# The last two blocks of a two-layer attention kernel: additions, residual, checks and GpSimd's drain rearranged

## The chip, the cores and the metric

The kernel runs on one core of a Trainium2 chip. The metric is the device time of one execution in microseconds (us), given as the median of several runs. Beside it stands one execution recorded by the hardware profiler: its span from the first to the last instruction, and every instruction and transfer in it.

A core has TensorE (PE, matrix products; its weight loads are listed as PEld), VectorE (DVE), ScalarE (ACT), GpSimd (POOL) and SyncE (SP). In this kernel SP does nothing but issue DMAs, and GpSimd mostly issues those DMAs that add to their destination.

## The reference

Input x has 16 images of 256 channels and 32 by 32 positions. Two layers follow each other, each adding attention to its input:

```python
x = x + attention_0(group_norm(x))
x = x + attention_1(group_norm(x))
```

In a layer, with 4 heads of 64 channels and n = 1024 positions:

```python
q, k, v = (W @ xf + b, split into heads)
sim  = einsum('bhdi,bhdj->bhij', q, k)
qpos = einsum('hdi,bhdj->bhij', rel_h + rel_w, q)
attn = softmax(sim + qpos, axis=-1)
out  = einsum('bhdn,bhmn->bhdm', v, attn)
```

All numbers are 32-bit floats.

## The kernel before, in words

**Units and blocks.** A unit is one layer of one image; there are 32 of them (list `units`). Each has two pairs of heads (`pr`), and each pair is done in two halves of 512 query positions. So there are 128 blocks `(u, pr, half)`, numbered n = 0 to 127. The last four are 124 and 125 (unit 31, pair 0; written 31_0 below) and 126 and 127 (unit 31, pair 1; 31_1). Unit 31 is layer 1 of image 15, and unit 30 that of image 14. In the traces 31_0 and 30_1 name such pairs.

**One block.** For each j of 8 tiles of keys, VectorE writes the position term into a PSUM tile (`seed`, L349), TensorE adds the product of q and k (`scores`, L385), and ScalarE writes the exponential to p (L394). For some tiles of the last blocks TensorE makes the position term too, out of `wide` (argument `tag` of `scores`), and no seed is needed. VectorE adds the eight p together (`add_up`, L403 for the first addition, L405 for the rest; the result is `acc`). TensorE multiplies v with p into `po` (`attend`, L419) in two stretches, `values_of_p(0)` and `values_of_p(1)`; between them GpSimd sets a token (L166) as a signal that the first stretch is done. ScalarE takes `po` out (`take_out`, L480).

**Sums.** The softmax's denominators are the sums of `acc` over its 128 rows. In most blocks GpSimd's adding DMAs fold them (L436, L441, L460, L465), and SP spreads the result into `den_all` (L473). In the last blocks TensorE sums the rows with a matrix of ones (`sums_of_p`, L490), ScalarE copies the sums into `d` (L500) and SP spreads them into `den_all` (L504). `reciprocals` then takes the reciprocals on VectorE (L515), sends them to DRAM (L517) and back, copied over 64 rows each (L522), into `rden`.

**The end of a pair.** `finish` multiplies the output with `rden` (`normalise`, L530) and adds bias and residual (`add_residual`, L537), both on VectorE; in layer 1 SP then stores the result (L539).

**Order.** The order of instructions on each engine is that of the program (a manual schedule): an engine runs its instructions in turn, and a waiting one holds all behind it. The order around the change is written out by hand in `block` and, for blocks 126 and 127, where no work on a next unit is left, in `block_without_pieces` (L758). PSUM tiles come from four tags `f0` to `f3`; a tile of a tag can be written when the reader of the one before is done.

**Block 126 before.** Additions 5 to 7 of block 125; scores 1 to 3; the sums of 31_0 (L772) and their spreading; reciprocals of 30_1 (`before`); the first additions, a seed for tile 7; scores 4 to 6 with `wide`; reciprocals of 31_0; first stretch of values; `finish` of 30_1; seeds for block 127, additions 5 and 6; second stretch of values.

**Block 127 before.** Addition 7 of block 126, the sums of block 126, `finish` of 31_0, additions, scores, first stretch of values; then the last addition, the sums over rows of this block into `pd` (L565), a reciprocal of all 512 columns at once (L813), the second stretch of values, sums over columns (L574) for the check, the second half of the output (L551, L552), then the checks.

**The checks.** `in_range` (L558 to L560) tests that all denominators lie between two bounds. The results go to `good`, are reduced to one number and written to `flag` (L822), which all engines load at L1194. If the flag says that a denominator was out of range, a general path runs instead (L1195, not taken here). L1223 is the line of the frame around the program: the drains and the barrier that end it.

Of the kernel before, what the change touches and what calls it, by code (L numbers as in the profile page):

```python
# [17 lines left out]
P = 128  # L18
# [34 lines left out]
def fast_path(ctx, tc, sh, x, layers, out, W, den_all, token, good, flag):  # L53
# [290 lines left out]
    def seed(blk, j, tag):  # L344

        u, pr, half = blk
        ps = psum2(tag, f"ps_{u}_{pr}_{half}_{j}")
        ab = abt[u, pr][:, :, j, :]
        nc.vector.tensor_tensor(  # L349
            ps.rearrange("p h (w y) -> p h w y", y=H),  # L350
            ab[:, :, :H].unsqueeze(2).to_broadcast([P, 2, XH, H]),
            ab[:, :, H + half * XH : H + (half + 1) * XH]
            .unsqueeze(3)
            .to_broadcast([P, 2, XH, H]),
            ALU.add,
        )
        seeds[blk, j] = ps
# [15 lines left out]
    def scores(blk, j, tag=None):  # L373

        u, pr, half = blk
        ps = psum2(tag, f"ps_{u}_{pr}_{half}_{j}") if tag else seeds.pop((blk, j))
        columns = slice(half * HALF, (half + 1) * HALF)
        for x, c in enumerate(QUARTERS):
            for h, hs in enumerate(QUARTERS):
                j0 = j * P + x * D  # L380
                terms = [(ks[u, pr], qs[u, pr])]
                if tag:
                    terms = [(qs[u, pr], wide[u, pr])] + terms
                for i, (a, b) in enumerate(terms):
# [12 lines left out]
    def add_up(blk, j):  # L397
        u, pr, half = blk
        if j == 0:
            return  # L400
        if j == 1:
            accs[blk] = apool.tile([P, 2, HALF], F32, tag="acc", name=f"acc_{u}_{pr}_{half}")
            nc.vector.tensor_tensor(accs[blk], probs[blk, 0], probs[blk, 1], ALU.add)  # L403
        else:
            nc.vector.tensor_tensor(accs[blk], accs[blk], probs[blk, j], ALU.add)  # L405
# [69 lines left out]
    def take_out(blk, po):  # L475

        u, pr, half = blk
        if half == 0:
            outs[u, pr] = opool.tile([P, 2, HALF], F32, tag="od", name=f"od_{u}_{pr}", bufs=3)
        nc.scalar.copy(  # L480
            outs[u, pr][:, half, :].rearrange("p (a n) -> p a n", a=2), po[:, :, :QUART]
        )

    def sums_of_p(two, po):

        for a in range(2):
            for x, blk in enumerate(two):
                for h in range(2):
                    r0 = (2 * x + h) * R
                    nc.tensor.matmul(  # L490
                        po[r0 : r0 + R, a, QUART:],
                        W.ones[:, :R],
                        accs[blk][:, h, a * QUART : (a + 1) * QUART],
                        start=True, stop=True, tile_position=(0, r0), skip_group_check=True,
                    )

    def keep_sums(po, n, count):
        rows_ = slice(0, 2 * count * R)
        d = ppool.tile([P, 2, HALF], F32, tag="p", name=f"d_{n}")[:, 0, :]
        nc.scalar.copy(d[rows_].rearrange("p (a n) -> p a n", a=2), po[rows_, :, QUART:])  # L500
        for x in range(count):
            for h in range(2):
                r0 = (2 * x + h) * R
                nc.sync.dma_start(  # L504
                    den_all[h * D : (h + 1) * D, n + x, :], d[r0 : r0 + 1, :]
                )

    def reciprocals(u, pr, count=2):

        n = index[u, pr, 0]
        r8 = fpool.tile([P, 2, 8], F32, tag="r8", name=f"r8_{u}_{pr}")
        nc.vector.reciprocal(r8[:, :count, :], den_all[:, n : n + count, :])  # L515
# [16 lines left out]
    def add_residual(u, pr):  # L532
# [5 lines left out]
        if l == NL - 1:  # L538
            nc.sync.dma_start(flat(out[b, pr * P : (pr + 1) * P]), xs)  # L539

    def finish(u, pr):
        normalise(u, pr)
        add_residual(u, pr)
# [15 lines left out]
        yield nc.vector.scalar_tensor_tensor(t, den, DEN_HI, t, ALU.is_le, ALU.mult)  # L559
        yield nc.vector.tensor_reduce(good[:, i : i + 1], t, AX.X, ALU.min)  # L560

    def sums_on_rows(acc, pd):

        for h, c in enumerate(QUARTERS):
            nc.tensor.matmul(  # L565
                pd[c, 0, :], W.ones[:, :D], acc[:, h, :],
                start=True, stop=True, skip_group_check=True,
            )

    def sums_on_columns(acc, pd):  # L570

        for h in range(2):
            for e in range(HALF // P):
                nc.tensor.matmul(  # L574
                    pd[:, 4 * h + e : 4 * h + e + 1],
                    acc[:, h, e * P : (e + 1) * P],
                    W.ones[:, :1],
                    start=True, stop=True, skip_group_check=True,
                )


# [37 lines left out]
    def block(n):  # L619
# [109 lines left out]
            spread_sums(*stacked)  # L729
        if half == 1 and u + 3 < NU and units[u + 3][1] == 0 and u > 0 or n == 3:  # L730
            load_x(units[u + 3][0], range(pr_, pr_ + 1) if u > 0 else range(CC))
        if half == 0:
            add_up(blk, 5)
        if before:
            finish(*before)
# [22 lines left out]
    def block_without_pieces(n, half):  # L758

        blk = blocks[n]  # L760
        u, pr, _ = blk
        f0, f1, f2, f3 = ring
        summed = blocks[n - 2][:2] if half == 0 else (u, pr)
        before = blocks[n - 4][:2] if half == 0 else blocks[n - 3][:2]
        first = index[summed + (0,)]
        if half == 0:
            add_up(blocks[n - 1], 5)
            add_up(blocks[n - 1], 6)
        add_up(blocks[n - 1], 7)
        for j in range(1, 4):  # L770
            scores(blk, j)
        sums_of_p(blocks[first:n], pos[n - 1])  # L772
        keep_sums(pos[n - 1], first, n - first)
        if half == 1:
            finish(*before)
        else:
            reciprocals(*before)
        add_up(blk, 1)
        seed(blk, 7, f2)
        add_up(blk, 2)  # L780
        add_up(blk, 3)
        for j, tag in ((4, f1), (5, f0), (6, f1)):
            scores(blk, j, tag)
        reciprocals(*summed, n - first)
        scores(blk, 7)
        add_up(blk, 4)
        if half == 0:
            seed(blocks[n + 1], 0, f0)
        po = pos[n] = psum2(f3, f"po_{n}")
        values_of_p = attend(blk, po)  # L790
        values_of_p(0)
        if half == 0:
            finish(*before)
            scores(blocks[n + 1], 0)
        if half == 0:
            seed(blocks[n + 1], 1, f1)
            seed(blocks[n + 1], 2, f2)
        add_up(blk, 5)
        if half == 0:
            seed(blocks[n + 1], 3, f0)  # L800
        add_up(blk, 6)
        if half == 0:
            values_of_p(1)
            take_out(blk, po)
            return
        add_up(blk, 7)
        acc = accs.pop(blk)
        pd = psum2(f0, "pd")
        sums_on_rows(acc, pd)
        values_of_p(1)  # L810
        finish_half(u, pr, 0, outs[u, pr][:, 0, :], rdens[u, pr][:, :HALF])
        rden = rdens[u, pr][:, HALF:]
        nc.vector.reciprocal(rden, pd[:, 0, :])  # L813
        pd = psum2(f2, "pd_columns")[:, 0, : 2 * HALF // P]
        sums_on_columns(acc, pd)
        finish_half(u, pr, 1, po[:, :, :QUART], rden)
        list(in_range(flatden[:, 8 * checked : 8 * n], 1))
        list(in_range(pd, 2))
        nc.vector.tensor_reduce(good[:, 3:4], good[:, 0:3], AX.X, ALU.min)
        pc = psum2(f1, "pc")[0:1, 0, 0:1]  # L820
        nc.tensor.matmul(pc, good[:, 3:4], W.ones[:, 0:1], start=True, stop=True)
        nc.vector.tensor_copy(flag, pc)  # L822
# [404 lines left out]
```

## Time and profile before

| What | us |
|---|---|
| Median of 3 runs | 2545.81 |
| Lowest and highest run | 2545.58, 2547.84 |
| The profiled execution | 2544.62 |
| Its span | 2542.9 |

Busy time in some stretches at the end, from the profile's sums by stretch:

| Stretch, us from the start | PE | DVE | ACT | POOL |
|---|---|---|---|---|
| 2440 to 2460 (20 long) | 20.00 | 18.70 | 10.80 | 6.91 |
| 2489 to 2510 (21 long, block 126) | 19.95 | 17.83 | 10.74 | 0.21 |
| 2510 to 2530 (20 long, block 127) | 16.09 | 19.48 | 7.77 | 0.09 |
| 2530 to 2543 (13 long) | 2.96 | 3.56 | 0.00 | 0.00 |

How to read the views: times are us from the start of the span. In the chain of waits a line is start, length, and what ran; "issue" is time in which nothing is waited for that the profile shows. In the timeline a line is start, length, engine, line of code, operation, output<-input, shape, count, and in brackets the idle time before it with what ended it. Drains, branches and waits for semaphores are run by an engine's sequencer (a q behind the engine's name) and aren't counted as busy. A matmul in fp32 is recorded as two.

### The profile page before, as it was taken

Reading aid. Unit: us, or ns where it says so; the run is one execution under the profiler, and the core shown is the slowest. Engines: PE = TensorE matmul, PEld = TensorE weight load, DVE = VectorE, ACT = ScalarE, POOL = GpSimd, SP = SyncE. Lnnn points to the kernel's source line nnn. Section 1 sums busy time; section 2 is a strip of 40 time slices with the busy share of each in tenths; the row PEclk is TensorE's granted clock in tenths of the full one; section 3 lists DMA queues with packets and bytes.
Section 4 is the critical chain, followed back from the end, with each engine's and each line's share of the span. In section 5 each row is a group of like instructions: output and inputs, shape, how many; then the busy total and the mean of one; then the engine's idle time right before and its main releaser. Section 6 shows DMA issues by size and latency. Waiting matters only on the chain.

```text
span 2542.9 us, 86134 instructions
## 1 busy us (share of the span) xinstructions
PE 2514.2 (99%) x37474; PEld 1335.6 (53%) x37474; DVE 2269.4 (89%) x2135; ACT 1949.5 (77%) x3874; POOL 835.1 (33%) x1194
## 2 busy tenths in 40 slices
PE   8999999999999999999999999999999999999997
PEld 4555555555555555555555555555555555555554
DVE  6888998989989889899898898998998998989997
ACT  6778777787777887777877778877778777787753
POOL 1332333323333233333233332333333333323320
PEclk9999999999999999999999999999999999999999
DMA  3344444454444444444444444445445444443441
GB/s 90 70 83 81 77 91 75 78 110 93 87 97 97 87 83 86 95 84 87 100 87 86 88 96 83 83 96 101 82 96 107 81 79 91 75 82 76 86 91 59
DMA packets 119537, 221.05 MB, mean 87 GB/s; under 512 B 53736, under 2 KB 55272, under 8 KB 119152
## 3 DMA queue, kind: packets, MB, share of 16 engines
q0 software_dynamic: 53568, 129.58, 30.7%
q1 hardware_dynamic: 65584, 85.90, 12.2%
q8 instruction: 295, 4.83, 0.8%
q14 instruction: 90, 0.74, 0.1%
HBM read 51.78 MB, written 17.30 MB: 27 GB/s over the span
## 4 chain that ended last, share of the span: by engine, by line
PE 94%; DVE 2%; POOL 1%; issue 1%; DMA 1%; SPq 0%; ACT 0%; POOLq 0%; DVEq 0%; ACTq 0%
PE po L419 33%; PE ps L385 33%; PE pv L298 8%; PE pk L268 8%; PE pq L268 8%; PE pa L326 2%; DVE acc L405 1%; DVE ps L349 1%; POOL rstd L237 1%; DMA stack<-stack 0%; POOL stack L465 0%; POOL stack L460 0%; PE pm L209 0%; DMA x<-in_x_dram 0%; DMA rden<-rd 0%
## 5 line engine op out<-in xcount | busy, mean ns | idle before, releaser
L349 DVE TENSOR_TENSOR ps<-abt 128x1024 f32<-128x1024 f32 x1018 | 1226.8, 1228 | 235.3 <-ACT p L394 147.7
L394 ACT ACTIVATE p<-ps,shift 128x1024 f32<-128x1024 f32 x1024 | 1092.2, 1114 | 323.4 <-PE ps L385 320.5
L385 PE MATMUL ps<-q,k 64*64 64x512 f32 x8192 | 985.5, 590 | 0.8 <-DVE ps L349 0.8
L419 PE MATMUL po<-p,v 64*64 64x256 f32 x16384 | 930.7, 376 | 2.1 <-POOL token L166 2.1
L419 PEld LDWEIGHTS po<-p,v 64*64 64x64 f32 x16384 | 628.9, 133 | 367.2 <-issue 76.9
L405 DVE TENSOR_TENSOR acc<-acc,p 128x1024 f32<-128x1024 f32 x644 | 783.3, 1216 | 7.1
L385 PEld LDWEIGHTS ps<-q,k 64*64 64x64 f32 x8192 | 308.5, 133 | 395.7 <-issue 275.1
L465 POOL DMA_DIRECT2D stack<-stack x310 | 249.6, 805 | 338.7 <-DMA stack<-stack 277.6
L166 POOL MEMSET token<- 1x1 f32 x320 | 35.8, 112 | 830.4 <-PE po L419 400.7
L460 POOL DMA_DIRECT2D stack<-acc x248 | 223.2, 1098 | 71.9 <-DMA stack<-acc 44.1
L298 PE MATMUL pv<-Wv,xn 64*64 64x256 f32 x4096 | 244.4, 376 | 1.6 <-POOL token L166 1.4
L268 PE MATMUL pq<-xn,Wq 64*64 64x512 f32 x2048 | 244.3, 592 | 0.3 <-DVE xn L913 0.3
L268 PE MATMUL pk<-xn,Wk 64*64 64x512 f32 x2048 | 242.8, 589 | 0.0
L248 ACT ACTIVATE xn<-x,nshift,rstd 128x128 f32<-128x128 f32 x496 | 209.9, 495 | 18.2 <-POOL nshift L239 18.2
L298 PEld LDWEIGHTS pv<-Wv,xn 64*64 64x64 f32 x4096 | 153.3, 133 | 104.3 <-issue 48.3
L190 ACT ACTIVATE junk<-x,neg 128x128 f32<-128x128 f32 x498 | 195.1, 401 | 0.0
L436 POOL DMA_DIRECT2D acc<-p x124 | 115.5, 931 | 227.8 <-ACT od L480 128.5
L441 POOL DMA_DIRECT2D acc<-acc x124 | 109.5, 883 | 206.0 <-DMA acc<-p 197.0
L480 ACT COPY od<-po 128x512 f32<-128x512 f32 x127 | 74.4, 586 | 118.9 <-PE po L419 118.9
L403 DVE TENSOR_TENSOR acc<-p,p 128x1024 f32<-128x1024 f32 x128 | 156.3, 1221 | 0.0
L268 PEld LDWEIGHTS pq<-xn,Wq 64*64 64x64 f32 x2048 | 78.6, 134 | 142.1 <-issue 136.7
L190 ACT ACTIVATE junk<-x 128x128 f32<-128x128 f32 x480 | 144.8, 311 | 0.0
(74 smaller groups left out, 1118.8 us busy)
## 6 DMA issues: line engine op xcount, KB each, us to landing
acc<-p POOLq DMA_DIRECT2D x124, 512.0 KB, 5.1
rden<-rd SPq DMA_DIRECT2D x126, 256.0 KB, 4.1
acc<-acc POOLq DMA_DIRECT2D x124, 256.0 KB, 3.6
x<-in_x_dram SPq DMA_DIRECT2D x32, 512.0 KB, 5.1
stack<-acc SPq DMA_DIRECT2D x248, 64.0 KB, 2.1
stack<-acc POOLq DMA_DIRECT2D x248, 64.0 KB, 3.3
out_dram<-x SPq DMA_DIRECT2D x31, 512.0 KB, 5.1
stack<-stack POOLq DMA_DIRECT2D x62, 128.0 KB, 2.9
```

The source lines that it names most:

```text
L190: nc.scalar.activation(junk, grouped(xt[units[u][0]], g), func, accum_out=into[:, g : g + 1], **bias)
L248: nc.scalar.activation(grouped(xns[u], g), grouped(xt[units[u][0]], g), AF.Identity, bias=shift[:, g : g + 1], scale=rstd[:, g : g + 1],)
L268: yield nc.tensor.matmul(pk[c, nh, :], w[l][rs, cc, c0 : c0 + D], xns[u][rs, cc, nh * HALF : (nh + 1) * HALF], start=(t == 0 and cc == 0), ...
L298: yield nc.tensor.matmul(pv[c, a, i, :], xns[u][rs, cc, j0 : j0 + D], W.wv[l][rs, cc, :], start=(t == 0 and cc == 0 and i == 0), stop=(t = ...
L349: nc.vector.tensor_tensor(ps.rearrange("p h (w y) -> p h w y", y=H), ab[:, :, :H].unsqueeze(2).to_broadcast([P, 2, XH, H]), ab[:, :, H + h ...
L385: nc.tensor.matmul(ps[c, h, :], a[hs, j0 : j0 + D], b[hs, columns], start=bool(tag) and i == 0, stop=i == len(terms) - 1, skip_group_check ...
L394: nc.scalar.activation(p, ps, AF.Exp, bias=W.shift)
L403: nc.vector.tensor_tensor(accs[blk], probs[blk, 0], probs[blk, 1], ALU.add)
L405: nc.vector.tensor_tensor(accs[blk], accs[blk], probs[blk, j], ALU.add)
L419: yield nc.tensor.matmul(po[c, a, :QUART], vts[u][rs, j, c0 : c0 + D], p[rs, h, a * QUART : (a + 1) * QUART], start=(t == 0 and j == 0), s ...
L460: nc.gpsimd.dma_start(at, acc[R:D, h, :], accum_op=ALU.add)
L465: nc.gpsimd.dma_start(stack[:rows_], stack[rows_ : 2 * rows_], accum_op=ALU.add)
```

## The change

All of it lies in `block_without_pieces`, but for one line in `block`; two small functions are new.

- **Block 125**: its addition 5 is made in the block itself, ahead of `finish`, and not at the start of block 126.
- **Block 126**: scores 4 stand ahead of the sums of 31_0. The reciprocals of 30_1 come first in SP's queue, then the spreading of the sums of 31_0 and its reciprocals. 30_1 is finished in another way: VectorE multiplies (`normalise`), ScalarE adds the bias to x in place, and a DMA issued by GpSimd adds the product to x (`add_by_dma`). Additions 5 to 7 of block 126 move to the start of block 127. After the DMA GpSimd runs a drain.
- **Block 127**: SP stores the x that the adding DMA completed (`store`). The checks of the denominators up to block 123 move to the start of the block. The last addition falls away: `sums_on_rows` takes `acc` and p of tile 7 and adds both on TensorE. `finish` of 31_0 moves behind the last addition. The sums over columns fall away: ScalarE copies `pd` into `d`, and SP spreads it into `den_all` by two DMAs, from where the last check reads blocks 126 and 127.

The built program's order shows besides that ScalarE's copy of `pd` waits for VectorE's reciprocal of `pd`, and that SP's store of x of image 14 stands between the spreading of the sums of block 126 and the reciprocals of 31_1.

```diff
+    def add_by_dma(u, pr):
+        b, l = units[u]
+        xs = xt[b][:, pr, :]
+        nc.scalar.activation(xs, xs, AF.Identity, bias=W.bv[l][:, pr : pr + 1])
+        nc.gpsimd.dma_start(xs, outs.pop((u, pr)).rearrange("p a n -> p (a n)"), accum_op=ALU.add)
+
+    def store(u, pr):
+        b = units[u][0]
+        nc.sync.dma_start(flat(out[b, pr * P : (pr + 1) * P]), xt[b][:, pr, :])
...
+    def sums_on_rows(parts, pd):
+        for i, part in enumerate(parts):
+            for h, c in enumerate(QUARTERS):
                 nc.tensor.matmul(
+                    pd[c, :], W.ones[:, :D], part[:, h, :],
+                    start=i == 0, stop=i == len(parts) - 1, skip_group_check=True,
                 )
...
-        if half == 0:
+        if half == 0 or n == len(blocks) - 3:
             add_up(blk, 5)
...
+        last = half == 1
+        previous = blocks[n - 1]
+        summed = previous[:2]
         first = index[summed + (0,)]
+        before = blocks[n - 4][:2]
+        for j in range(5 if last else 6, NT):
+            add_up(previous, j)
         for j in range(1, 4):
             scores(blk, j)
+        if last:
+            sums_of_p(blocks[first:n], pos[n - 1])
+            keep_sums(pos[n - 1], first, n - first)
+            store(*blocks[n - 5][:2])
+            list(in_range(flatden[:, 8 * checked : 8 * first], 1))
         add_up(blk, 1)
         seed(blk, 7, f2)
+        if not last:
+            reciprocals(*before)
         add_up(blk, 2)
         add_up(blk, 3)
+        scores(blk, 4, f1)
+        if last:
+            add_up(blk, 4)
+            reciprocals(*summed, n - first)
+        else:
+            sums_of_p(blocks[first:n], pos[n - 1])
+            keep_sums(pos[n - 1], first, n - first)
+        scores(blk, 5, f0)
+        scores(blk, 6, f1)
+        if last:
+            add_up(blk, 5)
+            add_up(blk, 6)
         scores(blk, 7)
         po = pos[n] = psum2(f3, f"po_{n}")
         values_of_p = attend(blk, po)
+        if not last:
+            after = blocks[n + 1]
+            seed(after, 0, f0)
+            add_up(blk, 4)
+            values_of_p(0)
+            scores(after, 0)
+            values_of_p.word()
+            seed(after, 1, f1)
+            seed(after, 2, f2)
+            reciprocals(*summed)
+            normalise(*before)
+            add_by_dma(*before)
+            seed(after, 3, f0)
             values_of_p(1)
+            nc.gpsimd.drain()
             take_out(blk, po)
             return
+        sums = (accs.pop(blk), probs[blk, NT - 1])
+        finish(*blocks[n - 2][:2])
+        values_of_p(0)
+        pd = psum2(f0, "pd")[:, 0, :]
+        sums_on_rows(sums, pd)
+        finish_half(u, pr, 0, outs[u, pr][:, 0, :], rdens[u, pr][:, :HALF])
+        values_of_p(1)
         rden = rdens[u, pr][:, HALF:]
+        nc.vector.reciprocal(rden, pd)
+        d = ppool.tile([P, 2, HALF], F32, tag="p", name=f"d_{n + 1}")[:, 0, :]
+        nc.scalar.copy(d, pd)
+        for hs in QUARTERS:
+            nc.sync.dma_start(den_all[hs, n, :], d[hs.start : hs.start + 1, :])
         finish_half(u, pr, 1, po[:, :, :QUART], rden)
+        list(in_range(flatden[:, 8 * (n - 1) :], 2))
         nc.vector.tensor_reduce(good[:, 3:4], good[:, 0:3], AX.X, ALU.min)
```

The lines taken away are those of `block_without_pieces` and of `sums_on_columns` as printed above, which the added lines replace.

More of the change, by code (lines that the diff above doesn't have):

```diff
@@ L560, in in_range @@
         yield nc.vector.tensor_reduce(good[:, i : i + 1], t, AX.X, ALU.min)
[L562 to L573, printed above, removed]
+    def sums_on_rows(parts, pd):
+        for i, part in enumerate(parts):
+            for h, c in enumerate(QUARTERS):
                 nc.tensor.matmul(
[L575 to L578, printed above, removed]
+                    pd[c, :], W.ones[:, :D], part[:, h, :],
+                    start=i == 0, stop=i == len(parts) - 1, skip_group_check=True,
                 )
@@ L762, in block_without_pieces @@
         f0, f1, f2, f3 = ring
-        summed = blocks[n - 2][:2] if half == 0 else (u, pr)
-        before = blocks[n - 4][:2] if half == 0 else blocks[n - 3][:2]
+        last = half == 1
+        previous = blocks[n - 1]
+        summed = previous[:2]
         first = index[summed + (0,)]
[L766 to L769, printed above, removed]
+        before = blocks[n - 4][:2]
+        for j in range(5 if last else 6, NT):
+            add_up(previous, j)
@@ L770, in block_without_pieces @@
         for j in range(1, 4):
             scores(blk, j)
[L772 to L777, printed above, removed]
+        if last:
[3 more added lines that the diff above has]
+            list(in_range(flatden[:, 8 * checked : 8 * first], 1))
         add_up(blk, 1)
@@ L779, in block_without_pieces @@
         seed(blk, 7, f2)
+        if not last:
+            reciprocals(*before)
         add_up(blk, 2)
         add_up(blk, 3)
-        for j, tag in ((4, f1), (5, f0), (6, f1)):
-            scores(blk, j, tag)
-        reciprocals(*summed, n - first)
+        scores(blk, 4, f1)
[6 more added lines that the diff above has]
+        scores(blk, 5, f0)
@@ L785, in block_without_pieces @@
+        scores(blk, 6, f1)
+        if last:
+            add_up(blk, 5)
+            add_up(blk, 6)
         scores(blk, 7)
-        add_up(blk, 4)
-        if half == 0:
-            seed(blocks[n + 1], 0, f0)
         po = pos[n] = psum2(f3, f"po_{n}")
         values_of_p = attend(blk, po)
[L791 to L802, printed above, removed]
+        if not last:
[11 more added lines that the diff above has]
+            seed(after, 3, f0)
@@ L803, in block_without_pieces @@
             values_of_p(1)
+            nc.gpsimd.drain()
             take_out(blk, po)
             return
[L806 to L809, printed above, removed]
+        sums = (accs.pop(blk), probs[blk, NT - 1])
[4 more added lines that the diff above has]
+        finish_half(u, pr, 0, outs[u, pr][:, 0, :], rdens[u, pr][:, :HALF])
         values_of_p(1)
-        finish_half(u, pr, 0, outs[u, pr][:, 0, :], rdens[u, pr][:, :HALF])
@@ L812, in block_without_pieces @@
         rden = rdens[u, pr][:, HALF:]
-        nc.vector.reciprocal(rden, pd[:, 0, :])
-        pd = psum2(f2, "pd_columns")[:, 0, : 2 * HALF // P]
-        sums_on_columns(acc, pd)
+        nc.vector.reciprocal(rden, pd)
[3 more added lines that the diff above has]
+            nc.sync.dma_start(den_all[hs, n, :], d[hs.start : hs.start + 1, :])
         finish_half(u, pr, 1, po[:, :, :QUART], rden)
-        list(in_range(flatden[:, 8 * checked : 8 * n], 1))
@@ L818, in block_without_pieces @@
-        list(in_range(pd, 2))
+        list(in_range(flatden[:, 8 * (n - 1) :], 2))
         nc.vector.tensor_reduce(good[:, 3:4], good[:, 0:3], AX.X, ALU.min)
```

## The prediction

> **What bounds the kernel now.** I read the page first (TensorE 99% busy, 94% of the chain), then the chain of waits in order of time for the last 60 us, then the timeline of the same stretch, and last the sequencers' instructions after the flag. Until 2467 the chain is TensorE alone, and the change leaves that part as it is. After that it goes over to VectorE and DMAs:
>
> ```profile
> 2493.61 1.08 PE po L490 x12
> ...
> 2494.76 0.59 ACT d L500
> ...
> 2497.86 1.60 DMA rd<-r
> ...
> 2499.98 3.99 DMA rden<-rd
> ...
> 2504.06 1.24 DVE od L530
> ...
> 2505.32 1.28 DVE x L537
> ...
> 2506.61 2.28 DVE ps L349 x2
> ```
>
> To be seen: in block 126 (the last but one) SP makes reciprocals for pair 31_0's sums before those of 30_1, so VectorE stands at od L530 for a landing, with four seeds and three additions queued behind it. The timeline shows what that costs TensorE, and what stands at the very end:
>
> ```profile
> 2513.69 1.06 PE L490 MATMUL po<-acc,ones 128*32 128x256 f32 x8 [1.39 <-DVE acc L405]
> ...
> 2520.84 5.21 DVE L405 TENSOR_TENSOR acc<-acc,p 128x1024 f32<-128x1024 f32 x4
> ...
> 2526.20 1.08 PE L565 MATMUL pd<-acc,ones 128*64 128x512 f32 x4 [1.72 <-DVE acc L405]
> 2527.21 3.68 PE L419 MATMUL po<-p,v 64*64 64x256 f32 x64
> 2527.36 3.35 DVE L813 RECIPROCAL rden<-pd 128x512 f32<-128x512 f32 x1
> ...
> 2534.15 0.15 DVE L822 CAST flag<-pc 1x1 int32<-1x1 f32 x1 [0.28 <-PE pc L821]
> ```
>
> Twice TensorE waits for VectorE's last addition. The flag is written at 2534.3, yet the span ends at 2542.9. That stretch is in the views of the two lines of code that end the program (durations in ns, then first and last start in us):
>
> ```profile
> L1223 POOLq DRAIN  x3: 44/107/6599, 2535.4 to 2542.6; - x3
> L1223 SPq DRAIN  x3: 7/7/7, 2539.4 to 2542.3; - x3
> ```
>
> ```profile
> L1195 PEldq COMPARE_BRANCH  x1: 4229/4229/4229, 2534.9 to 2534.9; - x1
> L1195 PEldq EVENT_SEMAPHORE  x1: 51/51/51, 2539.2 to 2539.2; - x1
> ```
>
> GpSimd's first drain runs from 2535.4 to 2542.0, and the closing barrier (0.8 to 0.9) comes after it. Everyone else is there at 2539.5: TensorE's branch takes 4.2, then its semaphore, then SP's drain. So the tail of 8.6 has two lanes, drain and branch, 2.6 apart.
>
> **What the Trainium skill says.** "VectorE: DVE Perf Modes", The DRAIN you can't avoid, puts the drains of a program's frame at about 12 ns on all five engines. Here SP's take 7, but GpSimd's last takes 6599 ns, so the measurement decides. "Runtime: NRT & Kernel Launch", Instruction fetch mechanics, says that a taken branch out of the fetched pages stalls for a fetch; that fits the 4.2 us of TensorE's branch, and it means that the change won't shorten it. "PSUM — Partial Sum Buffer", PSUM bank collisions raise a hardware error, has two engines kept apart on one bank, two readers too; the changed program's waits show it: the new copy of pd on ScalarE waits for VectorE's reciprocal of pd. "SBUF — State Buffer", SBUF: two separate sides, says that some VectorE operations lock GpSimd out of a shared port; no slowdown shows here (adding DMAs are issued in 0.88 to 0.93 us beside a busy VectorE), but it is the ground of a rival below.
>
> **The change part by part**, on the profiled execution's clock. A 128x1024 addition or seed takes 1.22 us; successive starts are 1.14 apart, 1.26 if the second needs the first, 1.33 if it needs ScalarE too (readings of the timeline).
>
> Block 125: its addition 5 moves ahead of L530 and L537. The seeds of 126 shift by 1.14; the last one ends at 2491.05 where TensorE wants it at 2490.96, which costs TensorE about 0.2. The last addition ends at 2493.4 as before (2493.55).
>
> Block 126: TensorE no longer waits from 2492.0 to 2493.6 for that addition, since scores 4 (1.75 us) come first: 2492.1 to 2493.9, the sums (about 1.45) to 2495.3, scores 5, 6 and 7 to 2499.6. Values begin at 2499.6 instead of 2500.65: 1.05 won. On VectorE the reciprocal of 30_1 runs at 2495.6, without its wait of 1.30. SP then sends rd (1.6) and the two rden, which land at about 2502, and behind them the four small transfers of d, which land at 2502.3 (1.8 after the last issue at 2500.5). VectorE meanwhile does additions 2 and 3, the seed of 127 at 2498.45 (it needs p5), addition 4 and two seeds, and comes to the reciprocal of 31_0 at 2503.0 and to L530 at 2503.2: both have landed, 0.7 and 1.2 to spare, and since seed 3 has to wait for p of 127 until 2505.3 anyway, 0.8 more. The stall of 1.61 goes. L537 goes too: ScalarE's Identity (1.1, in its idle time after 2505.3) and the adding DMA take its place. Then seed 3 from 2505.3 to 2506.5 and additions 5, 6, 7 to 2510.2. TensorE: values 0 to 2503.05, scores, values 1 to 2507.4, scores to 2510.0, sums from 2510.3 instead of 2513.69. **3.4 won** here, and TensorE waits 0.3 instead of 1.39.
>
> Block 127: TensorE runs 3.4 early through scores 4 to 7 and values 0, to 2520.85. VectorE: three checks (0.77) and then additions 1 to 4, with the reciprocal of 31_1 at 2516.9 instead of 2520.7, additions 5 and 6 to 2519.6. Addition 7 is gone: TensorE sums p7 itself (four more matmuls, 1.0 by the row of L565). L530 and L537 of 31_0, which before stood at 2513.5, now come here: 2519.55 to 2522.1. rden of 31_1 lands at 2522.1 (rd 1.4, issue 0.5, landing 3.0, as before), so L551's successor goes to 2522.9 and the residual to 2523.7. pd is ready at 2522.85. The reciprocal (3.35) runs from 2523.6 instead of 2527.36, to 2526.95: **3.75 won**. Values 1 end at 2526.5, just before it.
>
> From there the end is longer than before. Before, L551 and L552 followed (1.7), then seven small checks. Now the longer lane is ScalarE's copy (0.6, to 2527.6), two small DMAs (issued 0.55 apart, the second lands 1.8 to 2.4 after its issue: 2530.2), three checks, the last minimum, the product and the flag (1.25): **flag at 2531.5 against 2534.3, 2.8 won**. The earlier checks of 120 columns (0.77) and the 16 column products (1.95) are off the end. The two half stores lie beside this.
>
> SP's queue: the store of x_14 now waits for the adding DMA and stands ahead of rd of 31_1. The add is issued at 2507 and lands 5.1 later (4.5 to 9.5 over 124 of its kind), at 2512; rd is wanted at 2517. Covered by 5 us, and by 0.7 at its worst.
>
> GpSimd: the drain follows the adding DMA. It starts near 2508; with 6.6, plus at most the landing, it ends by 2519. Behind it on GpSimd is only the token of block 127, which values 1 need at 2522.85.
>
> The last drain is what the trace doesn't show after an early one. Lower bound: the second and third drains of the tail take 0.107 and 0.044, the one at the start 0.17, so the lane of TensorE's branch sets the end, at 6.0 after the flag: 2.6 won. Upper bound: it is 6.6 again, and nothing is won. I take the lower, because the long one comes 44 us after the last software DMA landed (it is no wait for a transfer) and because drains with none of those DMAs since the one before are short. A gain over 2.6 is excluded by the branch.
>
> **Sum**: 2.8 + 2.6 = 5.4. Profiled execution 2544.6 - 5.4 = 2539.2; the median of the runs is 1.2 above that execution, so 2540.4. What can be told from no change is 0.2%, 5.1 us, so this forecast lies just beyond it.
>
> **Rivals.** First, the last drain stays at 6.6, a fixed price of GpSimd's end: only 2.8 is won, 2543.0. For it: only one such drain is in the trace. Against: the short ones beside it. Second, the drain is short but the blocks win less, because a landing comes late: rden of 31_1 at its longest (6.4 instead of 3.0 after issue) or the small transfers queued behind a store's packets. L530's wait of 1.61 was of this kind. Each us of it is a us at the end; 1.5 lost gives 2541.9. Third, slower: the early drain, with VectorE busy beside it, becomes long and holds the token of block 127 in GpSimd's queue. From 2508 there are 15 us until values 1 are late; the checks by DMA hide 1.9 more and 5.4 are won elsewhere, so from a drain of 23 us the kernel is slower, and from 28 by more than 0.2%. A drain of 30 gives 2553. For it: the port lock of the SBUF page; against: the unhindered adding DMAs, and 6.6 when alone.
>
> **How the numbers follow.** Forecast 0.66, drain unchanged 0.17, late landing 0.10, long drain 0.07. About four fifths of the forecast's own spread (0.7 either way, and the branch allows no more in the tail) lie beyond 5.1: 0.53. Late landings of under 0.3 add 0.02. So faster 0.55, same 0.38, slower 0.07. The range, 2539.0 to 2543.4, takes in both bounds of the last drain and the late landing, and leaves out the long drain.
>
> **What would show it.** Right: no wait at od L530; sums of block 126 near 2510.3; the reciprocal of pd near 2523.6; flag near 2531.5; a drain of some 6 us in mid-kernel and one under 0.5 at the end; the last 6.0 us set by TensorE's branch. Wrong: a last drain over 4 us, a token of block 127 after 2523, or over 3.6 us between reciprocal and the checks of the last sums.

## The result, and the profile after

The changed kernel takes 2539.46 us (median of 17 runs, 2536.89 to 2546.61), the kernel before 2545.65 (17 runs): ratio 0.9978, 95% interval 0.997 to 0.9985, so 3.8 to 7.6 us won. The profiled execution took 2540.91, its span 2538.8.

A caution ahead of all that follows. The part that the change leaves alone does not take the same time in every execution: block 125's last value product ended 2489.42 us after the start in the profile before, 2491.73 in the one after, and up to 2495.1 in the other executions in which that part has the same instructions. So times near the end are counted below from that product (call it the mark). From there on they repeat better: the flag of the kernel before within 0.4 us over the four profiles that differ in GpSimd's drains alone, the sums of block 126 in the changed kernel within 0.01.

| us after the mark | before | after | won so far |
|---|---|---|---|
| values of block 126 begin | 11.23 | 9.81 | 1.42 |
| sums of block 126 | 24.27 | 20.59 | 3.68 |
| reciprocal of `pd` | 37.94 | 33.67 | 4.27 |
| flag | 44.73 | 41.30 | 3.43 |
| end | 53.44 | 47.10 | 6.34 |

The stretch won 6.3 us in this pair of profiles. Over all runs the ratio says 5.6 us (2545.65 x 0.0022), the difference of the two medians 6.2; the interval reaches from 3.8 to 7.6, so it stays open whether more than the prediction's 5.1 us is won.

The chain of waits after, from the end of block 126's first stretch of values on (start, length, what ran):

```profile
2505.24 0.88 PE ps L385 x8
...
2506.14 1.12 ACT p L394
...
2507.29 1.23 DVE ps L349
...
2508.52 1.14 DVE acc L405
...
2521.55 1.23 DVE od L530
...
2522.80 1.12 DVE x L537
...
2525.48 3.28 DVE rden L823
...
2528.84 0.59 ACT d L825
...
2529.98 1.80 DMA den_all<-d
```

To be seen: there is no landing of rd or rden in it any more. TensorE carries the chain until 2506, then it passes through ScalarE to a seed, and from there it is VectorE's to the end, but for the new lane of copy and small DMA. The timeline after shows the waits themselves (in brackets, the idle time before and its end):

```profile
2505.19 1.16 DVE L530 TENSOR_TENSOR od<-od,rden 128x1024 f32<-128x1024 f32 x1
...
2507.29 1.23 DVE L349 TENSOR_TENSOR ps<-abt 128x1024 f32<-128x1024 f32 x1 [0.94 <-ACT p L394]
...
2512.32 1.06 PE L490 MATMUL po<-acc,ones 128*32 128x256 f32 x8 [0.19 <-DVE range L568]
...
2525.40 3.35 DVE L823 RECIPROCAL rden<-pd 128x512 f32<-128x512 f32 x1
...
2528.84 0.58 ACT L825 COPY d<-pd 128x512 f32<-128x512 f32 x1 [7.87 <-DVE rden L823]
...
2531.88 0.17 DVE L568 TENSOR_SCALAR range<-den_all 128x16 f32<-128x16 f32 x1 [1.55 <-DMA den_all<-d]
...
2533.03 0.15 DVE L833 CAST flag<-pc 1x1 int32<-1x1 f32 x1 [0.37 <-PE pc L832]
```

L530 stands for nothing now; the seed behind it stands 0.94 for ScalarE, so VectorE has slack in block 126. TensorE waits 0.19 at the sums of block 126 instead of 1.39. At the end there is something new: ScalarE's copy waits for the whole reciprocal, and the last check waits 1.55 for the DMA behind it. And the drains and TensorE's branch, by their lines (ns, then first and last start):

```profile
L812 POOLq DRAIN  x1: 8256/8256/8256, 2508.6 to 2508.6; - x1
```

```profile
L1234 POOLq DRAIN  x3: 38/41/107, 2534.3 to 2538.6; - x3
```

```profile
L1206 PEldq COMPARE_BRANCH  x1: 3909/3909/3909, 2533.8 to 2533.8; - x1
```

The long drain has moved to 2508.6, and it is longer than before (8.26 us against 6.60); the one at 2534.3 takes 0.041. From flag to end it is 5.80 us instead of 8.71, and TensorE's branch, 2533.8 to 2537.7, is what sets it.

### The profile page after: what moved, and what is told of

It is laid out like the page before. It is cut to its first block, busy times and chain, and to the rows that moved or that the text cites. A ratio compares the mean times of both kernels' runs of the same rounds, so it can differ in the third digit from the quotient of the medians.

```text
span 2538.8 us, 86117 instructions
## 1 busy us (share of the span) xinstructions
PE 2512.0 (99%) x37462; PEld 1334.0 (53%) x37462; DVE 2266.0 (89%) x2133; ACT 1950.0 (77%) x3876; POOL 835.6 (33%) x1195
## 4 chain that ended last, share of the span: by engine, by line
PE 94%; DMA 2%; issue 1%; POOL 1%; DVE 1%; ACT 0%; SPq 0%; POOLq 0%; DVEq 0%; ACTq 0%
PE ps L385 33%; PE po L419 33%; PE pv L298 8%; PE pq L268 8%; PE pk L268 8%; PE pa L326 2%; DMA acc<-p 1%; POOL rstd L237 0%; DMA stack<-acc 0%; DMA acc<-acc 0%; POOL stack L465 0%; DMA stack<-stack 0%; DVE acc L405 0%; POOL stack L460 0%; PE pm L209 0%
```

## The experiments

The table gives each run's times after the mark, from one profiled execution each; the ratio is to the kernel before, run anew beside it, with its 95% interval. Two runs that were made only for the lengths of drains, one execution each (2548.01 and 2548.15 us), are left out here. A difference of 1 us is 0.04%, less than these intervals can tell, so the verdicts on the blocks rest on the profiles.

| Run | values 126 | sums 126 | reciprocal | flag | end | ratio |
|---|---|---|---|---|---|---|
| before | 11.23 | 24.27 | 37.94 | 44.73 | 53.44 | 1 |
| after | 9.81 | 20.59 | 33.67 | 41.30 | 47.10 | 0.9978 (0.997 to 0.9985) |
| without the drain | 9.82 | 20.59 | 33.82 | 41.45 | 50.25 | 0.9986 (0.9979 to 0.9992) |
| before, drain alone | 11.22 | 24.55 | 38.23 | 45.01 | 50.77 | 0.9989 (0.9983 to 0.9996) |
| copy first | 9.82 | 20.59 | 33.97 | 39.97 | 45.83 | 0.9968 (0.9955 to 0.9981) |
| added by VectorE | 9.82 | 20.96 | 34.06 | 41.70 | 47.82 | 0.9974 (0.9965 to 0.9983) |
| sums first | 11.11 | 21.92 | 35.00 | 42.63 | 48.62 | 0.998 (0.9974 to 0.9987) |
| last addition by VectorE | 9.82 | 20.59 | 35.00 | 42.62 | 48.77 | 0.9977 (0.9969 to 0.9985) |
| checks first | 9.81 | 20.59 | 33.96 | 38.46 | 45.10 | 0.9971 (0.996 to 0.9982) |
| reciprocals late | 9.81 | 21.35 | 34.59 | 42.22 | 48.08 | one execution |
| late and added by VectorE | 9.82 | 22.92 | 36.18 | 43.81 | 49.93 | one execution |
| checks first, drain in block 103 | 9.81 | 20.59 | 33.96 | 38.47 | 45.00 | 0.9994 (0.9985 to 1.0002) |

### The drain taken away, and the drain alone

```diff
-            nc.gpsimd.drain()
```

> The changed kernel without its early GpSimd drain. Theory (a drain is long when software DMAs were issued since the one before it): GpSimd's last drain is long again, 6.6 to 8.3 us as in the traces so far, so the stretch from the flag to the end goes back from 5.7 us to 8.5 or more, while the last two blocks stay as they are in the changed kernel (53.6 us before, 47.3 after, from scores 1 of block 126 to the end; here about 50.2). Against the kernel before only the blocks' part of the gain is left: about 3.4 us, ratio near 0.9987. Rival (the last drain became short for another reason, such as the fewer semaphores or DMAs around the end, or the later adding DMA): the last drain stays under 0.2 us and the time is that of the changed kernel, ratio 0.9978.

The other way round, that line was put at the same place of the kernel before, ahead of `take_out` of block 126.

> The kernel before with nothing but one early GpSimd drain at the end of block 126. Theory: this drain takes about 6.6 us (no adding DMA is in flight there, the last software DMA landed some 20 us earlier), hidden, because only the token of block 127 stands behind it on GpSimd; the last drain takes under 0.2 us; the flag stays where it is, and from the flag to the end it is 5.7 to 6.0 us instead of 8.6: 2.6 to 2.9 us won, ratio near 0.9989. Rival 1 (the price is one of the program's end): the last drain stays at 6.6, ratio 1.000. Rival 2 (an early drain is long in proportion to what is in flight, 8.26 us in the changed kernel with the adding DMA pending): here it is well under 6 us.

GpSimd's drains in the frame of the first, and both drains of the second (its own, then those of the frame):

```profile
L1233 POOLq DRAIN  x3: 44/107/6687, 2537.3 to 2544.5; - x3
```

```profile
L804 POOLq DRAIN  x1: 6724/6724/6724, 2505.2 to 2505.2; - x1
```

```profile
L1224 POOLq DRAIN  x3: 38/44/107, 2536.4 to 2540.6; - x3
```

Without the early drain the last one is 6.69 us again and the end 8.8 us after the flag; with it alone the last one is 0.044 and the end 5.8 after the flag, the flag being where it was within 0.3. No software DMA was in flight in the second (the last had landed 14 us ahead), and its early drain took 6.7 us all the same, so the rival on what is in flight falls as the sole cause, and so does that of a price of the end. Both runs gave what the theory expected. The two parts also sum up: 0.9986 and 0.9989 leave 0.9975 for both, and 0.9978 was measured.

### The residual by VectorE again

```diff
-            store(*blocks[n - 5][:2])
...
-            normalise(*before)
-            add_by_dma(*before)
+            finish(*before)
```

> The changed kernel with the residual of pair 30_1 added by VectorE again (one operation of 1.28 us in block 126, stored at once), in place of ScalarE's Identity and the adding DMA. Theory (VectorE stood 0.94 us for ScalarE's p at seed 3 there, so most of the addition is hidden): sums of block 126 come 0.3 to 0.4 us later, and so does the end; ratio near 0.9979. Rival (VectorE is the bound of block 126 and each of its operations counts whole): 1.2 us later, ratio 0.9983. On the drain: it has no adding DMA in flight now. If its 8.26 us contained a wait for that DMA it falls to about 6.6; if not, it stays at 8.3. The last drain stays under 0.2 us.

Sums 0.37 later, flag 0.40: the theory's number. An operation of 1.28 cost 0.4, since the rest lay in the 0.94 that VectorE would have waited (its wait at the seed is gone with it). Its early drain, with no DMA in flight:

```profile
L810 POOLq DRAIN  x1: 6724/6724/6724, 2503.5 to 2503.5; - x1
```

So the adding DMA, whose issue is recorded 0.02 after the drain's start, made it longer by 1.5 in the changed kernel. By the expectation this means that the 8.26 held a wait for that DMA; more on it below.

### The reciprocals of 30_1 late again, alone and with the addition

```diff
-        if not last:
-            reciprocals(*before)
...
             keep_sums(pos[n - 1], first, n - first)
+            reciprocals(*before)
```

> The changed kernel with only the order of the small transfers in block 126 undone: the reciprocals of pair 30_1 come after the sums of 31_0 are kept, so that rd and rden stand behind four small DMAs in SP's queue. Theory (the landing of rden then holds VectorE at od L530 by 0.5 to 1.0 us, but seed 3 behind it waits 0.94 us for ScalarE's p anyway): a wait at L530, yet sums of block 126 and flag at most 0.3 us later (flag 41.3 to 41.6 us after the end of block 125's values). Rival (the stall of 1.6 us in the kernel before was worth its length and comes back): 1.3 to 1.6 us later.

The second of the two has the edit of the previous section besides.

> The run before and the addition by VectorE together: in block 126 both the wait for rden and VectorE's addition L537 (1.28 us) are back. Theory (the slack of 0.94 us is used up by the first of them, so the two don't add up as alone): 1.3 to 1.8 us later than the changed kernel at the sums of block 126 and at the flag (42.6 to 43.1 us after the end of block 125's values), although the two alone cost 0.4 and at most 0.3. Rival (their costs add): at most 0.7 us later.

The product with rden in block 126, in the timeline of the first and of the second:

```profile
2508.89 1.22 DVE L530 TENSOR_TENSOR od<-od,rden 128x1024 f32<-128x1024 f32 x1 [1.61 <-DMA rden<-rd]
```

```profile
2510.55 1.23 DVE L530 TENSOR_TENSOR od<-od,rden 128x1024 f32<-128x1024 f32 x1 [1.84 <-DMA rden<-rd]
...
2511.82 1.28 DVE L537 SCALAR_TENSOR_TENSOR x<-od,bv,x 128x1024 f32<-128x1024 f32 x1
```

The stall came back at its old length of 1.61, not at the 0.5 to 1.0 that both my numbers were made from. It is not quite the old stall: the edit also puts VectorE's reciprocal behind two additions, and L530 starts 15.19 and 15.43 us after the mark, against 14.64 in the kernel before. Alone it cost 0.76 at the sums and 0.92 at the flag: between the theory's 0.3 and the rival's 1.3, and near what 1.61 less some 0.9 of slack gives. Both together cost 2.33 at the sums and 2.51 at the flag, more than the 1.8 expected, for the same reason; alone they cost 0.92 and 0.40, which add to 1.32. That they don't add as alone is the theory's point, and it holds: the first to come uses up the slack, the second counts whole. (The second run's stall is 1.84, so 0.23 of the 1.59 that the addition cost at the flag there is a later landing.)

### The sums first again

```diff
+        if not last:
+            sums_of_p(blocks[first:n], pos[n - 1])
+            keep_sums(pos[n - 1], first, n - first)
         scores(blk, 4, f1)
         if last:
             add_up(blk, 4)
             reciprocals(*summed, n - first)
-        else:
-            sums_of_p(blocks[first:n], pos[n - 1])
-            keep_sums(pos[n - 1], first, n - first)
```

> The changed kernel with TensorE's order of block 126 undone: the sums of pair 31_0 (which need VectorE's last addition of block 125) ahead of scores 4 again. Theory (block 126 is bound by TensorE now, VectorE stands 0.94 us there for ScalarE's p): TensorE waits about 1.6 us for the addition again, values of 126 begin 1.0 to 1.4 us later, and the rest with them until the flag; from the end of block 125's values to the flag 42.3 to 42.7 us instead of 41.3; ratio near 0.9982. Rival (VectorE's chain sets block 126 and had the slack): under 0.3 us lost, ratio 0.9978.

In its timeline TensorE makes four of the sums and then stands for the addition:

```profile
2497.24 0.63 PE L490 MATMUL po<-acc,ones 128*32 128x256 f32 x4
...
2498.61 1.06 PE L490 MATMUL po<-acc,ones 128*32 128x256 f32 x12 [0.74 <-DVE acc L405]
```

Values of 126 begin 1.30 later, sums of 126 and flag 1.33 later: TensorE's time in that block counts whole. This 1.33 and the 2.33 of stall and addition come to 3.66, near the 3.68 won in block 126, but that is no account of the 3.68: no run has all three undone, the stall came back at another place than in the kernel before, and VectorE's order of seeds and additions, which changed too, was not tried alone. Each run says what one part is worth within the changed kernel.

### The last addition by VectorE again

```diff
         scores(blk, 7)
+        if last:
+            add_up(blk, 7)
...
-        sums = (accs.pop(blk), probs[blk, NT - 1])
+        sums = (accs.pop(blk),)
```

> The changed kernel with the last addition of block 127 on VectorE again (1.2 us), and TensorE's sums over the one accumulator (4 matmuls fewer, 1.0 us less). Theory (from od L530 on VectorE works without a gap up to the reciprocal of pd, so its additions count whole): reciprocal and flag 1.1 to 1.2 us later, ratio near 0.9983. Rival 1 (TensorE sets the time of the reciprocal): pd is ready up to 1.0 us sooner, 0 to 1.0 us won, ratio 0.9974 to 0.9978. Rival 2 (the end is set by the landing of the last sums alone): no change in the flag.

`pd` is ready 1.1 us after its first matmul starts, and VectorE comes to it 2.5 us after that:

```profile
2521.08 1.08 PE L576 MATMUL pd<-acc,ones 128*64 128x512 f32 x4
...
2524.03 0.75 DVE L562 SCALAR_TENSOR_TENSOR x<-od,bv,x 128x512 f32<-128x512 f32 x1
...
2524.70 3.35 DVE L825 RECIPROCAL rden<-pd 128x512 f32<-128x512 f32 x1
```

Reciprocal and flag come 1.33 and 1.32 later (1.1 to 1.2 expected). VectorE is the bound from L530 on. This also tells what else block 127 does: between sums and reciprocal 0.59 were won in all (13.67 to 13.08), so the remainder of its changes cost 0.74. The three moved checks take 0.8 there in the changed kernel (from 2512.09); that they are the cost is my reading, it was not tried alone.

### The copy first

```diff
+        d = ppool.tile([P, 2, HALF], F32, tag="p", name=f"d_{n + 1}")[:, 0, :]
+        nc.scalar.copy(d, pd)
         nc.vector.reciprocal(rden, pd)
-        d = ppool.tile([P, 2, HALF], F32, tag="p", name=f"d_{n + 1}")[:, 0, :]
-        nc.scalar.copy(d, pd)
```

> The changed kernel with ScalarE's copy of pd put ahead of VectorE's reciprocal of pd, so that the small DMAs of the last sums lie beside the reciprocal. Theory (after the reciprocal the lane of copy, two DMAs and their landing sets the end; the range check waits 1.55 us for it): the copy takes 0.6 us from 2524.9, the reciprocal starts at most 0.2 us later than now, the landing comes near 2528.5, before VectorE is through its last two products, and the wait of 1.55 us is gone: flag 1.3 to 1.6 us earlier, and the whole 1.3 to 1.6 us shorter than the changed kernel, 7 us or so below the one before, ratio near 0.9972. Rival 1 (the copy comes later than pd is ready, or the reciprocal waits for all of it): the reciprocal is 0.6 us later, 1.0 us won. Rival 2 (the store of the last half or another lane holds the end): flag earlier but nothing won, ratio 0.9978.

In its timeline the last check follows VectorE's own product without a wait:

```profile
2525.95 0.58 ACT L824 COPY d<-pd 128x512 f32<-128x512 f32 x1 [4.11 <-PE pd L576]
...
2526.57 3.36 DVE L825 RECIPROCAL rden<-pd 128x512 f32<-128x512 f32 x1
...
2531.43 0.17 DVE L568 TENSOR_SCALAR range<-den_all 128x16 f32<-128x16 f32 x1
```

The reciprocal is 0.30 later, the flag 1.33 earlier, the end 1.27 earlier. So some 1.6 of the changed kernel's end was the lane of copy and DMA behind the reciprocal; the 0.30 is uncertain, since in the run without the drain, which has the reciprocal first too, it is 0.15 later as well.

### The checks first

The copy first as above; besides, the two DMAs of `d` ahead of the store of the first half, and the end in this order:

```diff
-        finish_half(u, pr, 1, po[:, :, :QUART], rden)
...
         list(in_range(flatden[:, 8 * (n - 1) :], 2))
         nc.vector.tensor_reduce(good[:, 3:4], good[:, 0:3], AX.X, ALU.min)
...
         nc.tensor.matmul(pc, good[:, 3:4], W.ones[:, 0:1], start=True, stop=True)
+        nc.vector.tensor_tensor(y[:, 1, :], o, rden[:, right], ALU.mult)
         nc.vector.tensor_copy(flag, pc)
+        nc.vector.scalar_tensor_tensor(xs[:, right], y[:, 1, :], bias, xs[:, right], ALU.add, ALU.add)
```

> The changed kernel with three edits to its end: ScalarE's copy ahead of the reciprocal as in the run on that edit, the two small DMAs of the last sums ahead of the first half's store in SP's queue, and the last checks ahead of the last two products, of which one fills the wait for TensorE and one comes after the flag. Theory (after the reciprocal only VectorE's own work is left on the path): the sums land before the reciprocal is over, the flag is 1.0 us earlier than with the copy alone, 2.3 us earlier than in the changed kernel (39.0 us after the end of block 125's values instead of 41.3), and the end 0.8 us earlier than with the copy alone, since VectorE now comes as late as TensorE's branch; ratio near 0.9965. Rival (the landing still sets the checks, or the last store holds the end): the flag or the end no earlier than with the copy alone, ratio 0.9972.

```profile
2528.00 0.11 DVE L568 TENSOR_SCALAR range<-den_all 128x16 f32<-128x16 f32 x1
...
2528.64 0.68 DVE L838 TENSOR_TENSOR od<-po,rden 128x512 f32<-128x512 f32 x1
...
2528.87 0.19 PE L837 MATMUL pc<-ones,good 128*1 128x1 f32 x2 [1.24 <-DVE good L835]
...
2529.23 0.13 DVE L839 CAST flag<-pc 1x1 int32<-1x1 f32 x1
```

The flag is 2.84 earlier than in the changed kernel (2.3 expected), the end 2.00 earlier. The last store, behind the flag now, lands when TensorE's branch ends (2533.97 and 2533.95), and SP, which waits for it, has 1.0 us of further waits for semaphores behind it; that is why the end wins less than the flag. Against the kernel before the ratio is 0.9971 (0.996 to 0.9982), about 7.4 us; the stretch after the mark says that it beats the changed kernel, too, but the intervals of the two overlap, so by the times alone that stays open.

### What makes a drain long

Three kernels with more drains. In the first, five in the kernel before:

```diff
         values_of_p(1)
+        if n in (4, 64, 124, 125):
+            nc.gpsimd.drain()
         take_out(blk, po)
...
+            nc.gpsimd.drain()
```

> The kernel before with five GpSimd drains, at the ends of blocks 4, 64, 124, 125 and 126; one look at their durations. Between them lie some 20, 480, 480, 5 and no software DMAs. Theory (a fixed price for a drain that has had at least one software DMA since the one before, a little more where one is in flight): the drains of blocks 4, 64, 124 and 125 each take 6.6 to 8.3 us, that of 126 and the last of the program under 0.2. Rival 1 (the price grows with the number of software DMAs since the last drain): block 4 and block 125 take far less than 6 us, 64 and 124 more than half of 6.7. Rival 2 (the first drain of a program pays once, for its code): only that of block 4 is long. Rival 3 (it is paid after a long time without a drain): 64 and 124 long, 125 short. In every case the last drain is short and the end is 5.7 to 6.1 us after the flag; the blocks with a drain may lose a few us.

Its drains in order of time (blocks 4, 64, 124, 125 and 126):

```profile
L749 POOLq DRAIN  x1: 7122/7122/7122, 132.4 to 132.4; - x1
L749 POOLq DRAIN  x1: 6011/6011/6011, 1302.9 to 1302.9; - x1
L749 POOLq DRAIN  x1: 4867/4867/4867, 2474.6 to 2474.6; - x1
L749 POOLq DRAIN  x1: 2412/2412/2412, 2495.0 to 2495.0; - x1
L806 POOLq DRAIN  x1: 178/178/178, 2511.2 to 2511.2; - x1
```

The software DMAs begun since the drain before were 20, 390, 390, 5 and 1. The first, with the fewest but two, is the longest: it goes neither by their number nor by a fixed price, and theory and the first two rivals fall. The third, the time without a drain, isn't excluded here: after 14 and 15 us they took 0.18 and 2.41, after 132 to 1166 us 4.87 to 7.12. The next run excludes it: there 14 us gave 5.55 and 438 us gave 1.64. From flag to end it is 5.46 here and 5.60 in the next run, the last drain being 0.05 in both.

In the second the drains stood at the starts of blocks 0 and 1, ahead of the first software DMA, and at the ends of blocks 100 to 103 and 126.

> The kernel before with drains at the starts of blocks 0 and 1 (ahead of the first software DMA), at the ends of blocks 100, 101, 102 and 103 (18 us and 6 to 8 software DMAs apart) and at the end of block 126. The look with five drains gave 7.1, 6.0, 4.9, 2.4 and 0.2 us, so neither a fixed price nor one by the number of software DMAs holds. Theory (a drain is long only where software DMAs came since the one before, and longer where more than a block of them did): blocks 0 and 1 under 0.3 us, 100 5 to 7, 101 to 103 1.5 to 2.5 each, 126 4 to 6. Rival 1 (each drain of a program is shorter than the one before, whatever lies between): block 0 6 to 7, block 1 less, block 100 under 5, falling to under 1 at 103 and 126. Rival 2 (the time since the last drain decides): 0 and 1 under 1, as above for 100, but 101 to 103 under 0.3.

The four in blocks 100 to 103 and that of 126:

```profile
L751 POOLq DRAIN  x1: 7646/7646/7646, 2005.3 to 2005.3; - x1
L751 POOLq DRAIN  x1: 2588/2588/2588, 2028.9 to 2028.9; - x1
L751 POOLq DRAIN  x1: 5552/5552/5552, 2045.8 to 2045.8; - x1
L751 POOLq DRAIN  x1: 1597/1597/1597, 2071.7 to 2071.7; - x1
L808 POOLq DRAIN  x1: 1641/1641/1641, 2511.3 to 2511.3; - x1
```

The software DMAs since the drain before were 644, 9, 4, 10 and 139. The two ahead of all software DMAs took 3.65 (GpSimd's own operation, begun 0.02 after it, ran 3.55 of that) and 0.16, and they did not shorten the first one after. Again none of the three theories holds as put. What the two runs share: the first drain behind software DMAs is the longest, 7.1 and 7.6, be they 20 or 644; one with none between is under 0.2, or with the one that began 0.02 after the start of the drain before and landed ahead of its end; and a later one is shorter even after 139. The last was tried in the third kernel, which is the run with the checks first, its drain moved to the end of block 103.

> The run with the checks first, with its one early drain moved from block 126 to the end of block 103, so that some 140 software DMAs follow it. In the look at drains by gap the drain of block 126 took 1.6 us after 139 software DMAs since the one before, though that was the fifth drain of its kernel. Theory (one early drain takes most of the price away, wherever it stands and whatever follows it): 6 to 8 us in block 103, the last one 1.5 to 2.0 us, which lies beside TensorE's branch of 4; from the end of block 125's values to the end 45 us as with the drain in block 126, ratio near 0.9968. Rival 1 (only the repeated drains made the later ones short): the last drain takes 5 to 6.7 us again and the end comes 1.5 to 2.7 us later, ratio near 0.9977. Rival 2 (a drain of 7 us in a block that still needs GpSimd's adding DMAs holds TensorE's work): the last drain is short, but 1 us or more is lost around block 104.

Its early drain, the drains of the frame, and its timeline in block 104:

```profile
L749 POOLq DRAIN  x1: 5952/5952/5952, 2066.1 to 2066.1; - x1
```

```profile
L1243 POOLq DRAIN  x3: 50/107/1612, 2537.2 to 2542.2; - x3
```

```profile
2072.61 0.95 POOL L436 DMA_DIRECT2D acc<-p  x1 [5.76 <-issue]
...
2073.26 0.48 POOL L166 MEMSET token<- 1x1 f32 x2
...
2073.66 3.69 PE L298 MATMUL pv<-Wv,xn 64*64 64x256 f32 x32 [3.91 <-POOL token L166]
```

The last drain is 1.61 after 140 software DMAs, as the theory had it, and the end is 45.00 after the mark, no later than with the drain in block 126. But the second rival came true: the tokens stood behind the drain in GpSimd's queue, TensorE waited for them, and block 104 took 27.42 us, against 20.66 in the kernel before. These 6.8 us take back nearly all (ratio 0.9994).

The traces of all these runs say more, though no run was made for it. Beside 13 of the early drains the issue of a software DMA was recorded 0.02 to 0.14 us after the drain's start, so that its transfer was under way. All 13 ended after that transfer had landed, by 0.2 to 3.4 us. In the six kernels with the adding DMA of block 126 the drain ended 3.35 us behind the landing each time, while that landing came 4.85 to 6.49 us after the issue. Shown are the time from issue to landing of that DMA in the changed kernel, then the drain and that time in the run with the reciprocals late, where both are longest:

```profile
DMA to landing us min/median/max: 4.9/4.9/4.9
```

```profile
L811 POOLq DRAIN  x1: 9871/9871/9871, 2510.7 to 2510.7; - x1
```

```profile
DMA to landing us min/median/max: 6.5/6.5/6.5
```

A landing 1.6 later made the drain 1.6 longer. So the drain held for a transfer under way, by these traces. This also puts the later drains in order, which their number of software DMAs does not: with a transfer under way they took 2.4 to 6.0, with all landed 1.6 (after 10, 139 and 140) or under 0.2. What a drain does beyond that wait, 6.0 to 6.7 us in a first one with all landed and 1.6 in a later one, stays open.

## Why the prediction was right

Ratio and median fell near the forecast (2540.4 predicted, 2539.46 measured), and the steps hold when counted from the mark.

- **Block 126, "3.4 won"**: 3.68. The values of 126 begin 1.42 earlier (1.05 predicted; the sums took 1.07, not 1.45). That seed 3 would wait for ScalarE anyway was seen (0.8 put, 0.94 measured); by the runs, stall and addition are worth 0.92 and 0.40 at the flag alone, and 2.51 together. Two readings of the kernel before were off, without effect on the sum: behind L530 stood three seeds, not four, and ahead of 30_1's reciprocals SP's queue had the spreading of 31_0's sums, not its reciprocals. The spare time was tighter than put: rden had 1.07 to spare (1.2 predicted), but the small transfers of d landed at 2504.79 for a reciprocal at 2505.03, 0.24 to spare instead of 0.7.
- **Block 127, "3.75 won"** at the reciprocal: 4.27, VectorE being the bound as assumed.
- **The longer end, "2.8 won"** at the flag: 3.43. The lane from reciprocal to flag took 7.78 to the flag's end, for the 7.9 put; it gives back 0.84 of what the blocks won, and the run with the copy first shows that its wait on the reciprocal is to blame. What the column products and the earlier checks gave by leaving the end was not tried alone.
- **The drain, "2.6 won"**: 2.91. The mechanism is shown by taking the drain away and by setting it alone. The excess is mostly the branch, 3.91 instead of 4.23. "6.6 plus at most the landing" was 8.26, and it ended 6.4 us before GpSimd was wanted. That a drain "is no wait for a transfer" holds for the one at the end, 45 us after the last landing; the early one did hold for the adding DMA.
- **The rivals**: the drain at the end stayed short. The price of a late landing, "each us of it is a us at the end", was too high for block 126: 1.61 cost 0.92. Half of the slower rival's mechanism is real: a drain does hold the token behind it, as block 104 shows, but in the changed kernel there were 14.7 us from the drain's start to the next token. The other half, that a busy VectorE makes the drain long, did not show: it took 6.72 beside a busy VectorE and 6.60 and 6.69 at the end.

The sum, 5.4, stands against 6.34 in the profiles after the mark, 5.6 by the ratio and 6.2 by the medians. Every term was a little low, by 0.6 for the flag and 0.3 for the tail. That the median fell within 1 us of the forecast is in part luck: the part ahead of the mark differs by up to 5.7 us between executions, and in the profile after it took 2.3 longer than in the one before, which is most of why that execution took 2540.91 instead of the 2539.2 put, though its end won more.

## What to carry to other kernels

Look at what stands between the last useful instruction and the end of the span: a long drain of GpSimd there can be paid earlier, beside other work, if no signal stands behind it in GpSimd's queue. A wait and an operation on the same engine share one slack, so price them together and not one by one. When a result is needed by two readers, ask which of them has the longer way to the end, and let that one read first.

## What the runs showed of the hardware

- The first GpSimd drain behind software DMAs took 6.0 to 7.6 us, 45 us after the last landing (6.60) as well as just behind an issue, and 8.2 to 9.9 with the adding DMA of block 126 under way. A later one took under 0.2 with nothing new to wait for, 1.6 with 10 to 140 software DMAs between, all landed, and 2.4 to 6.0 with one under way. All 13 drains with a transfer under way ended after its landing. "VectorE: DVE Perf Modes", The DRAIN you can't avoid, puts the drains of a program's frame at about 12 ns; that was so for the other engines (7 to 17 ns, once 130), not for GpSimd.
- TensorE's branch around the general path took 3.58 to 4.26 us over all profiles, always the longest of the five engines; ScalarE's and VectorE's took 0.05 and 0.07, but their next instruction came 2.4 to 3.5 us later. Why TensorE's is the longest no run shows.
- Counted from the mark, the sums of block 126 came at 20.59 us in each of the six kernels that have the changed block 126 unaltered but for the drain, while the mark itself lay between 2489.42 and 2495.12 us over the executions with no drain added ahead of it.
